# A cross-network kernel on one core: V2 spread by one-row transfers, M written in runs of 8 KB, the vectors in one load, chunk 1 loaded ahead of W2

## The chip, the core and the metric

The kernel runs on one core of a Trainium2 chip. The metric is device time in microseconds (us) of one execution. The six runs of the kernel before lie within 0.7% of each other. The span of a profile is a little shorter than the time (515.9 against 517.7 us in the profiled run of the kernel before, which was the fastest of its six). The profile counts 16 DMA engines on the core, which carry the transfers that SP (SyncE), ACT and POOL issue; a "DMA share" is the mean busy share of the 16, and a transfer has landed when its completion is reported. A run whose clock was throttled throughout is called slow, and such runs are not compared with others.

## The reference

A three-layer compressed interaction network over 1024 rows of 64 features and 16 embedding positions. Each layer multiplies every feature with every hidden channel and contracts the 64 x 64 products with a weight matrix:

```python
h = x0 = x                                   # [1024, 64, 16]
for i in range(3):
    z = einsum('bfe,bge->bfge', x0, h).reshape(B, 64 * 64, 16)
    y = einsum('oc,bce->boe', W[i], z) + b[i][None, :, None]     # 128 channels
    if i != 2: x_i, h = y[:, :64], y[:, 64:]
    else:      x_i = y
    xs.append(x_i)
out = sum(concatenate(xs, 1), 2) @ fc_w.T + fc_b
```

The kernel does not compute the third layer as such: only its weighted sum is wanted. It folds fc_w into W2, which gives a 64 x 64 matrix V2 (one matmul row over all of W2), folds V2 into W1, which gives M, a 64 x 64 x 64 tensor, and uses M, with its two feature axes added symmetrically, as 64 more weight columns beside those of layer 1. All is float32.

## The kernel before

TensorE (PE) contracts, VectorE (DVE) makes the products z, ScalarE (ACT) copies and squares. A chunk is 32 rows of the batch. V2 and M are made while chunks 0 to 3 run their first half (`half_contract(c, 0, j)`, the columns from W0); the second half (`half_contract(c, 1, j)`) needs the columns from M. The parts that matter:

```python
    # start: loads, all on SP's queue; eight semaphores for DMAs in turn
    load_xa(0); ...xw[0], xw[1]...            # chunk 0 and W0, 3 MB
    for k in range(2):
        nc.sync.dma_start(out=w2s[k], in_=w2t[k])      # W2, 2 x 1 MB
    load_chunk(1)                                      # 2 MB
    nc.sync.dma_start(out=w1s, in_=w1h)                # W1, 1 MB
    load_chunk(2)
    # ... 13 small loads of vectors on POOL (GpSimd)
    for j in range(2):
        half_contract(0, 0, j)
    load_chunk(3)
    # V2: column sums of W2 weighted with fc_w, on 4 partitions (0, 32, 64, 96)
    ...
    for to in halves:                                  # two transfers of 16 KB: 4 partitions -> 64, twice
        nc.scalar.dma_start(
            out=v2t[to],
            in_=v2r[0:128:32].rearrange("k n (o f) -> k (n o) f", f=F),
        )
    for j in range(2, NJ + 1):
        half_contract(0, 0, j)
    # ... chunk 1, first two tiles
    # M = V2 x W1, in m_sb [128, 4, 512]; written to memory as md[f1, f2, g], with wrapped copies of rows and columns
    def quarter(rows, first):
        return md[rows, first : first + 16, :].rearrange("r (m f) g -> r m (f g)", m=2)
    for n in range(2):
        at = 64 * n
        f0 = 16 * n
        nc.scalar.dma_start(out=quarter(slice(0, 64), f0), in_=m_sb[halves[n], n::2, :])
        nc.scalar.dma_start(out=quarter(slice(0, 64), 32 + f0), in_=m_sb[halves[1 - n], n::2, :])
        nc.sync.dma_start(out=quarter(slice(32, 64), 64 + f0), in_=m_sb[at + 32 : at + 64, n::2, :])
        nc.sync.dma_start(out=quarter(slice(64, 96), 32 + f0), in_=m_sb[64 - at : 96 - at, n::2, :])
        ...
    # ... chunks 2 and 3, first half
    # read back skewed (row f1 starts at column f1), in 1 KB and 256 B pieces, half on SP, half on ACT
    for half in range(2):
        ...
    nc.vector.tensor_tensor(w_all[:, 0:NT, 64:128], ms[:, 0], ms[:, 1], ALU.add)   # the weights from M
    load_chunk(4)
    for c in range(2, NF):                             # second half of chunks 2 and 3
        for j in range(NJ):
            half_contract(c, 1, j)
```

## Time and profile before

| | before |
|---|---|
| time, median of 6 runs | 519.22 us (517.73 to 520.98) |
| span of the profiled run | 515.9 us |
| PE busy | 495.8 us, 96% |
| PE idle at the start / for chunk 1 / for V2 / for the weights from M | 10.87 / 2.12 / 2.41 / 0.20 us |
| first weights from M used | 55.61 us |

A line of the chain view is a start, a duration and a piece of work; the chain is followed back from the last instruction, so a piece on it delayed the end. A line of an engine's timeline adds the matmul's shapes and, in brackets, how long the engine had been idle and what released it. PE counts each float32 matmul as two records, hence "x32" for 16 instructions. Lines such as L180 are lines of the kernel; the changed kernel has other line numbers for the same statements (L198 became L178, L302 became L275, L367 became L336, L159 became L139). The lines of this profile stand in the prediction below.

### The profile page before, as it was taken

To read this page: it belongs to the slowest core of one execution; us is meant where nothing else is said; L and a number is where in the kernel's file an instruction comes from. 1 tells how busy PE (TensorE), PEld (TensorE's weight loads), DVE (VectorE), ACT (ScalarE), POOL (GpSimd) and SP (SyncE) were. 2 spreads that over 40 slices of the span, in tenths; PEclk is the share of its full clock that TensorE was granted. 3 is DMA by queue.
4 is the path that set the end of the run, shared out by engine and by line. 5 is a ranking of instruction groups with operands and counts; after the bars stand their busy time and mean duration, and the time that the engine had idled before them with its cause. 6 is when DMAs were issued, how large, how long until landed. Compare 5 with 4: busy or idle time off the path is not lost.

```text
span 515.9 us, 3854 instructions
## 1 busy us (share of the span) xinstructions
PE 495.8 (96%) x1576; PEld 229.9 (45%) x1576; DVE 370.3 (72%) x224; ACT 81.5 (16%) x141; POOL 8.1 (2%) x23
## 2 busy tenths in 40 slices
PE   1889999999999999999999999999999999999996
PEld 0446754444544444444444444444444444444432
DVE  3698499999999995849577584957758495771103
ACT  1113114021311101111110111111011111100001
POOL 6000000000000000000000000000000000000000
PEclk9989999999999999999999999999999999999999
DMA  7977995344456544442324444232444421000000
GB/s 284 415 305 177 348 424 223 151 175 164 163 217 238 198 164 163 163 163 96 129 102 163 163 165 163 98 128 100 163 163 163 164 105 57 0 1 1 0 0 0
DMA packets 15167, 80.66 MB, mean 156 GB/s; under 512 B 4194, under 2 KB 4750, under 8 KB 5806
## 3 DMA queue, kind: packets, MB, share of 16 engines
q1 hardware_dynamic: 12626, 78.73, 39.6%
q10 hardware_dynamic: 2108, 1.61, 1.4%
q8 instruction: 12, 0.20, 0.1%
q0 software_dynamic: 416, 0.09, 0.1%
q14 instruction: 5, 0.04, 0.0%
HBM read 78.74 MB, written 1.64 MB: 156 GB/s over the span
## 4 chain that ended last, share of the span: by engine, by line
PE 93%; DMA 4%; DVE 1%; ACTq 1%; ACT 0%; issue 0%; SPq 0%; DVEq 0%
PE acc L180 75%; PE acc L198 9%; PE acc L185 5%; PE y L227 3%; DMA v2t<-v2r 3%; DMA xw<-in_xw 1%; DMA ms<-md 1%; DVE z L159 0%; PE pv L267 0%; PE pm L302 0%; PE po L431 0%; ACTq L360 0%; DVE w_all L367 0%; ACTq L274 0%; DVE uu L223 0%
## 5 line engine op out<-in xcount | busy, mean ns | idle before, releaser
L180 PE MATMUL acc<-z,w_all 128*128 128x512 f32 x896 | 392.0, 593 | 0.0
L159 DVE TENSOR_TENSOR z<-xa,xb 128x2048 f32<-128x2048 f32 x132 | 295.7, 2285 | 37.1 <-PE acc L180 28.3
L180 PEld LDWEIGHTS acc<-z,w_all 128*128 128x128 f32 x896 | 169.9, 190 | 214.0 <-issue 209.2
L198 PE MATMUL acc<-z,w_all 128*64 128x256 f32 x512 | 61.5, 400 | 13.2 <-DVE w_all L242 10.9
L222 ACT COPY q<-acc 64x512 f32<-64x512 f32 x28 | 16.3, 582 | 309.8 <-PE acc L185 309.4
L198 PEld LDWEIGHTS acc<-z,w_all 128*64 128x64 f32 x512 | 39.7, 144 | 35.6 <-DVE w_all L242 10.9
L230 DVE SCALAR_TENSOR_TENSOR uu<-y,cx,xx 128x512 f32<-128x512 f32 x16 | 11.9, 746 | 56.4 <-PE y L227 56.4
L223 DVE SCALAR_TENSOR_TENSOR uu<-acc,bh,q 64x512 f32<-64x512 f32 x28 | 20.7, 740 | 35.3 <-ACT q L222 34.8
L185 PE MATMUL acc<-zl,w_all 128*128 128x512 f32 x56 | 28.6, 592 | 0.0
L166 ACT ACTIVATE zl<-xa 64x512 f32<-64x512 f32 x34 | 21.3, 628 | 25.2 <-PE acc L198 17.7
L175 ACT COPY xx<-xa 64x512 f32<-64x512 f32 x32 | 19.6, 614 | 20.2 <-DVE uu L230 19.8
L234 DVE TENSOR_REDUCE acc<-uu 128x64 f32<-128x1024 f32 (+2 forms) x18 | 20.2, 1129 | 0.6
L171 ACT COPY zl<-xa 64x512 f32<-64x512 f32 x32 | 19.7, 615 | 0.4
L185 PEld LDWEIGHTS acc<-zl,w_all 128*128 128x128 f32 x56 | 10.6, 190 | 13.4 <-issue 13.4
L227 PE MATMUL y<-xx,bd 128*128 128x512 f32 x32 | 16.3, 595 | 0.0
L159 DVE TENSOR_TENSOR z<-xa,xw 128x2048 f32<-128x2048 f32 x4 | 9.1, 2285 | 8.2 <-DMA xw<-in_xw 8.2
L227 PEld LDWEIGHTS y<-xx,bd 128*128 128x128 f32 x32 | 6.0, 190 | 7.6 <-issue 7.6
L302 PE MATMUL pm<-w1s,v2t 64*64 64x512 f32 x16 | 3.0, 605 | 2.4 <-DMA v2t<-v2r 2.4
L437 ACT ACTIVATE res<-po,cst 2x480 f32<-2x480 f32 (+1 forms) x2 | 0.9, 465 | 25.2 <-PE po L431 25.2
L198 PE MATMUL acc<-zl,w_all 64*64 64x256 f32 (+1 forms) x32 | 4.9, 393 | 0.0
L204 ACT ACTIVATE hb<-acc,bh 128x256 f32<-128x256 f32 x4 | 1.9, 474 | 17.4 <-PE acc L198 17.4
L431 PE MATMUL po<-acc,ones 128*2 128x480 f32 (+1 forms) x8 | 2.2, 379 | 2.0 <-DVE acc L234 2.0
(46 smaller groups left out, 36.7 us busy)
## 6 DMA issues: line engine op xcount, KB each, us to landing
xa<-in_xra SPq DMA_DIRECT2D x34, 1024.0 KB, 4.7
xb<-in_xrb SPq DMA_DIRECT2D x33, 1024.0 KB, 7.2
w<-in_w2t SPq DMA_DIRECT2D x2, 1024.0 KB
xw<-in_xw SPq DMA_DIRECT2D x2, 512.0 KB, 8.2
xw<-in_xw SPq DMA_DIRECT2D x1, 1024.0 KB
w1s<-in_w1h SPq DMA_DIRECT2D x1, 1024.0 KB
md<-m_sb ACTq DMA_DIRECT2D x4, 256.0 KB, 5.1
w1x<-in_wx SPq DMA_DIRECT2D x1, 1024.0 KB, 9.9
```

The costliest lines, as they stand in the source:

```text
L159: nc.vector.tensor_tensor(z, xas[c], xbs[c][j].unsqueeze(1).to_broadcast([128, NI, N]), ALU.mult)
L166: nc.scalar.activation(zls[c][0:64], xas[c][0:64, 0, :], AF.Square)
L171: nc.scalar.copy(zls[c][64:128], xas[c][64:128, 0, :])
L175: nc.scalar.copy(xxs[c // 2][to], xas[c][to, 0, :])
L180: nc.tensor.matmul(accs[c], w_all[:, t, :], zs[c, j][:, i, :], start=(t == 0), stop=False)
L185: nc.tensor.matmul(accs[c], w_all[:, NT, :], zls[c], start=False, stop=True)
L198: nc.tensor.matmul(accs[c][halves[n]], w_all[rows, t, cols], z[rows, n * H2 : (n + 1) * H2], start=(t == 0), stop=(t == NT),)
L222: nc.scalar.copy(q, accs[c][64:128])
L223: nc.vector.scalar_tensor_tensor(uu, accs[c][0:64], bh1[0:64], q, ALU.add, ALU.mult)
L227: nc.tensor.matmul(ys[k], bd, xxs[k], start=True, stop=True)
L230: nc.vector.scalar_tensor_tensor(uus[k][:, 1, :], ys[k], cx, xxs[k], ALU.add, ALU.mult)
L234: nc.vector.tensor_reduce(acc[rows, parts, k, :], uus[k][rows, parts].rearrange("p k (b e) -> p k b e", e=E), AX.X, ALU.add,)
```

## The change

The intent: V2 reaches the other partitions sooner, by transfers that each use every DMA engine; M is laid out so that it leaves in runs of 8 KB with few transfers; thirteen small loads become one; and chunk 1 comes ahead of W2, so that PE has work. W1 is permuted on the host to suit. The core of the diff (the host's packing, the PE order of M's matmuls and the renaming of the read-back are cut):

```diff
-    nc.gpsimd.dma_start(out=fc2, in_=fc_w[0, 128:256].unsqueeze(1))
-    ...twelve more
+    vs = const_tile("vs", [128, NV])
+    nc.scalar.dma_start(out=vs, in_=vec)
...
+    load_chunk(1)
     for k in range(2):
         nc.sync.dma_start(out=w2s[k], in_=w2t[k])
-    load_chunk(1)
     nc.sync.dma_start(out=w1s, in_=w1h)
...
-    for j in range(2):
+    for j in range(NJ + 1):
         half_contract(0, 0, j)
+    keep_h1(0)
+    squares(1)
     load_chunk(3)
...
-    for to in halves:
+    for k in range(4):
         nc.scalar.dma_start(
-            out=v2t[to],
-            in_=v2r[0:128:32].rearrange("k n (o f) -> k (n o) f", f=F),
-        )
+            out=v2t[16 * k : 16 * k + 16],
+            in_=v2r[32 * k : 32 * k + 1].rearrange("k n (o f) -> k (n o) f", f=F),
+        )
+    nc.scalar.copy(v2t[halves[1]], v2t[halves[0]])
...
-    for j in range(2):
+    for j in range(3):
         half_contract(1, 0, j)
...
+    def m_ap(f1, f2, dims):
+        return bass.AP(tensor=md.tensor, offset=md.offset + f1 * row + f2 * F, ap=dims)
+    m_rows = m_sb.rearrange("p m c -> p (m c)")
+    nc.scalar.dma_start(out=m_ap(0, 0, [[32 * F, 2], [row, F], [1, 32 * F]]), in_=m_rows)
     nc.sync.dma_start(
-        out=md[68:96, 64:68, :].rearrange("r f g -> r (f g)"), in_=m_sb[4:32, 0, 0:256]
+        out=m_ap(32, 64, [[32 * row - 32 * F, 2], [row, 32], [1, 32 * F]]), in_=m_rows[32:96]
     )
+    nc.sync.dma_start(out=m_ap(64, 64, [[row, 4], [1, 32 * F]]), in_=m_rows[0:4])
+    nc.sync.dma_start(out=m_ap(68, 64, [[row, 28], [1, 4 * F]]), in_=m_rows[4:32, 0 : 4 * F])
```

In the read-back, the last small transfer moves from SP's queue to ACT's, and ACT's part comes ahead of its wait for chunk 2.

More of the change, by code (lines that the diff above doesn't have):

```diff
@@ L46, with cin_kernel @@
 NF = 4
+NV = 200
 @with_exitstack
-def cin_kernel(ctx, tc, xra, xrb, xw0, xw1, w0d, w1h, w2t, wx1, wx0, b0, b1, b2, fc_w, fc_b, out):
+def cin_kernel(ctx, tc, xra, xrb, xw0, xw1, w1h, w2t, wx1, wx0, vec, out):
     nc = tc.nc
@@ L70, in set_tile @@
         return setup.tile([128, NI * N], F32, tag="set", name=name)
-    fc2 = const_tile("fc2", [128, 1])
-    bh1 = const_tile("bh1", [128, 1])
-    bh2 = const_tile("bh2", [F, 1])
-    bcol = const_tile("bcol", [128, 2])
-    fcol = const_tile("fcol", [128, 2])
-    fcb = const_tile("fcb", [2, 1])
-    fcr = const_tile("fcr", [128, 128])
-    w0ds = const_tile("w0ds", [F, F])
-    b0c = b0.unsqueeze(1)
-    b1c = b1.unsqueeze(1)
-    nc.gpsimd.dma_start(out=fc2, in_=fc_w[0, 128:256].unsqueeze(1))
-    nc.gpsimd.dma_start(out=w0ds, in_=w0d)
-    for to in halves:
-        nc.gpsimd.dma_start(out=bh1[to], in_=b0c[64:128])
-    nc.gpsimd.dma_start(out=bh2, in_=b1c[64:128])
-    nc.gpsimd.dma_start(out=bcol[0:64, 0:1], in_=b0c[0:64])
-    nc.gpsimd.dma_start(out=bcol[64:128, 0:1], in_=b1c[0:64])
-    nc.gpsimd.dma_start(out=bcol[:, 1:2], in_=b2.unsqueeze(1))
-    for n in range(2):
-        nc.gpsimd.dma_start(
-            out=fcol[:, n : n + 1], in_=fc_w[0, n * 128 : (n + 1) * 128].unsqueeze(1)
-        )
-        nc.gpsimd.dma_start(out=fcb[n : n + 1], in_=fc_b.unsqueeze(1))
-    nc.gpsimd.dma_start(
-        out=fcr, in_=bass.AP(tensor=fc_w.tensor, offset=0, ap=[[0, 128], [1, 128]])
-    )
+    vs = const_tile("vs", [128, NV])
+    nc.scalar.dma_start(out=vs, in_=vec)
+    fc2, bh1, bh2 = vs[:, 0:1], vs[:, 1:2], vs[0:64, 2:3]
+    bcol, fcol, fcb = vs[:, 3:5], vs[:, 5:7], vs[0:2, 7:8]
+    w0ds, fcr = vs[0:64, 8:72], vs[:, 72:200]
     fv2 = const_tile("fv2", [128, 32])
-    nc.gpsimd.tensor_copy(fv2, fc2.to_broadcast([128, 32]))
+    nc.scalar.copy(fv2, fc2.to_broadcast([128, 32]))
     ones = const_tile("ones", [128, 2])
@@ L272, in cin_kernel @@
         nc.scalar.copy(v2r[:, n, :], pv)
-    for to in halves:
+    for k in range(4):
         nc.scalar.dma_start(
-            out=v2t[to],
-            in_=v2r[0:128:32].rearrange("k n (o f) -> k (n o) f", f=F),
-        )
-    for j in range(2, NJ + 1):
-        half_contract(0, 0, j)
-    keep_h1(0)
-    squares(1)
+            out=v2t[16 * k : 16 * k + 16],
+            in_=v2r[32 * k : 32 * k + 1].rearrange("k n (o f) -> k (n o) f", f=F),
+        )
+    nc.scalar.copy(v2t[halves[1]], v2t[halves[0]])
     new_acc(1, H2)
@@ L286, in cin_kernel @@
         product(1, j)
-    for j in range(2):
+    for j in range(3):
         half_contract(1, 0, j)
     m_sb = z_tile("m_sb")
-    pms = []
-    for m in range(0, NI, 2):
-        pms += [
-            ps.tile([128, N], F32, tag=("set", "y")[m // 2], name=f"pm_{m + n}") for n in range(2)
-        ]
+    pms = [ps.tile([128, N], F32, tag=("set", "y")[m // 2], name=f"pm_{m}") for m in range(NI)]
+    for m in (0, 1):
         for n in range(2):
             for h in range(2):
-                e = 2 * n + m // 2
@@ L302, in cin_kernel @@
                 nc.tensor.matmul(
-                    pms[m + n][halves[h ^ n]], v2t[halves[h]],
-                    w1s[halves[h], e * N : (e + 1) * N], start=True, stop=True,
-                )
-        for n in range(2):
-            nc.scalar.copy(m_sb[:, m + n, :], pms[m + n])
+                    pms[m + 2 * n][halves[h ^ n]], v2t[halves[h]],
+                    w1s[halves[h], (m + 2 * n) * N : (m + 2 * n + 1) * N], start=True, stop=True,
+                )
+    for m in range(NI):
+        nc.scalar.copy(m_sb[:, m, :], pms[m])
@@ L311, in cin_kernel @@
     md = dr.tile([EXT, EXT, F], F32, tag="md", name="md")
-    def quarter(rows, first):
-        return md[rows, first : first + 16, :].rearrange("r (m f) g -> r m (f g)", m=2)
-    for n in range(2):
-        at = 64 * n
-        f0 = 16 * n
-        nc.scalar.dma_start(out=quarter(slice(0, 64), f0), in_=m_sb[halves[n], n::2, :])
-        nc.scalar.dma_start(out=quarter(slice(0, 64), 32 + f0), in_=m_sb[halves[1 - n], n::2, :])
-        nc.sync.dma_start(out=quarter(slice(32, 64), 64 + f0), in_=m_sb[at + 32 : at + 64, n::2, :])
-        nc.sync.dma_start(out=quarter(slice(64, 96), 32 + f0), in_=m_sb[64 - at : 96 - at, n::2, :])
-        nc.sync.dma_start(out=quarter(slice(64, 68), 64 + f0), in_=m_sb[at : at + 4, n::2, :])
+    row = EXT * F
@@ L324, in cin_kernel @@
+    def m_ap(f1, f2, dims):
+        return bass.AP(tensor=md.tensor, offset=md.offset + f1 * row + f2 * F, ap=dims)
+    m_rows = m_sb.rearrange("p m c -> p (m c)")
+    nc.scalar.dma_start(out=m_ap(0, 0, [[32 * F, 2], [row, F], [1, 32 * F]]), in_=m_rows)
     nc.sync.dma_start(
-        out=md[68:96, 64:68, :].rearrange("r f g -> r (f g)"), in_=m_sb[4:32, 0, 0:256]
+        out=m_ap(32, 64, [[32 * row - 32 * F, 2], [row, 32], [1, 32 * F]]), in_=m_rows[32:96]
     )
-    for j in range(2, NJ + 1):
+    nc.sync.dma_start(out=m_ap(64, 64, [[row, 4], [1, 32 * F]]), in_=m_rows[0:4])
@@ L328, in cin_kernel @@
+    nc.sync.dma_start(out=m_ap(68, 64, [[row, 28], [1, 4 * F]]), in_=m_rows[4:32, 0 : 4 * F])
+    for j in range(3, NJ + 1):
         half_contract(1, 0, j)
@@ L339, in cin_kernel, with skewed @@
             half_contract(c, 0, j)
-    keep_h1(2)
-    ms = set_tile("ms").rearrange("p (v t g) -> p v t g", v=2, g=F)
-    row = EXT * F
-    def skewed(first, dims):
-        return bass.AP(
-            tensor=md.tensor, offset=md.offset + first, ap=[[row + F, F]] + dims
-        )
-    for half in range(2):
-        to = halves[half]
-        b = 16 * half + 4
-        queue = (nc.sync, nc.scalar)[half]
-        queue.dma_start(
-            out=ms[to, 0].rearrange("p (j i) g -> p j (i g)", i=NI),
-            in_=skewed(b * row, [[4 * row, NJ], [1, NI * F]]),
-        )
-        for i in range(NI):
-            queue.dma_start(
-                out=ms[to, 1].rearrange("p (j i) g -> p j i g", i=NI)[:, :, i, :],
-                in_=skewed(i * row + b * F, [[4 * F, NJ], [1, F]]),
-            )
-    nc.sync.dma_start(out=w_all[0:64, NT, 64:128], in_=skewed(0, [[1, F]]))
+    ms = set_tile("ms").rearrange("p (v t g) -> p v t g", v=2, g=F)
+    def skewed(f1, f2, dims):
+        at = len(dims) - 2
+        return m_ap(f1, f2, dims[:at] + [[row + F, F]] + dims[at:])
+    for half in range(2):
+        (nc.sync, nc.scalar)[half].dma_start(
+            out=ms[halves[half], 0].rearrange("p (j i) g -> p j (i g)", i=NI),
+            in_=skewed(16 * half + 4, 0, [[4 * row, NJ], [1, NI * F]]),
+        )
+    for i in range(NI):
+        for half in range(2):
+            queue = (nc.sync, nc.scalar)[half]
+            queue.dma_start(
+                out=ms[halves[half], 1].rearrange("p (j i) g -> p j i g", i=NI)[:, :, i, :],
+                in_=skewed(i, 16 * half + 4, [[4 * F, NJ], [1, F]]),
+            )
+    nc.scalar.dma_start(out=w_all[0:64, NT, 64:128], in_=m_ap(0, 0, [[row + F, F], [1, F]]))
+    keep_h1(2)
     keep_h1(3)
@@ L518 @@
     xw = np.stack([xrb[0], w0p], axis=2)
+    w1q = w1[64:].reshape(64, 2, 2, 16 * F)
+    w1q = np.stack([w1q[:, :, 0], w1q[:, ::-1, 1]], axis=2).transpose(1, 0, 2, 3).reshape(128, 32 * F)
+    b0, b1, b2 = (np.asarray(b) for b in (L0_rec_b0, L0_rec_b1, L0_rec_b2))
+    fc = np.asarray(L0_rec_fc_w)[0]
+    vec = np.concatenate([
+        np.stack([
+            fc[128:], np.tile(b0[64:], 2), np.tile(b1[64:], 2), np.concatenate([b0[:64], b1[:64]]),
+            b2, fc[:128], fc[128:], np.full(128, np.asarray(L0_rec_fc_b)[0]),
+        ], axis=1),
+        np.tile(w0[64:, np.arange(F), np.arange(F)].T, (2, 1)),
+        np.tile(fc[:128], (128, 1)),
+    ], axis=1)
     def summed(w):
@@ L528 @@
         "xw1": xw[:, 2:].reshape(128, 4, N),
-        "w0d": w0[64:, np.arange(F), np.arange(F)].transpose(1, 0),
-        "w1h": w1[64:].reshape(64, 2, 32 * F).transpose(1, 0, 2).reshape(128, 32 * F),
+        "w1h": w1q,
         "w2t": w2.transpose(0, 2, 1).reshape(128, 4, 2, 8 * F).transpose(2, 0, 1, 3).reshape(2, 128, 32 * F),
@@ L533 @@
         "wx0": summed(w0[:64]),
-        "b0": np.asarray(L0_rec_b0),
-        "b1": np.asarray(L0_rec_b1),
-        "b2": np.asarray(L0_rec_b2),
-        "fc_w": np.asarray(L0_rec_fc_w),
-        "fc_b": np.asarray(L0_rec_fc_b),
+        "vec": vec,
     }
```

## The prediction

> **What bounds the kernel now.** I read the page first, then the chain that ended last in order of time, the timeline of TensorE (PE), the waits, the time windows of the stretch that changes, and the DMA issues. On the page PE is busy 96% of the span: 495.8 of 515.9 us. The 20.1 us left are four gaps and the tail. The chain, where it passes through the stretch that the change touches:
>
> ```profile
> 1.19 6.89 DMA xw<-in_xw
> 8.18 2.29 DVE z L159
> ...
> 10.87 6.09 PE acc L198 x32
> 16.97 2.01 PE pv L267 x16
> 19.00 0.59 ACT v2r L272
> 19.62 1.15 ACTq L274
> 20.80 13.16 DMA v2t<-v2r
> 34.01 1.94 PE pm L302 x14
> 35.95 11.85 PE acc L198 x104
> ...
> 50.79 3.13 DMA ms<-md
> 54.24 1.24 DVE w_all L367
> 55.61 14.03 PE acc L198 x128
> ```
>
> First column is the start, second the duration. The only long piece that isn't PE work is the 13.16 us transfer of 2 x 16 KB of V2. The timeline of PE shows what of this PE really lost:
>
> ```profile
> 22.47 0.65 PE L198 MATMUL acc<-zl,w_all 64*64 64x256 f32 x4
> 25.25 5.36 PE L198 MATMUL acc<-z,w_all 128*64 128x256 f32 x32 [2.12 <-DVE z L159]
> 30.54 1.07 PE L302 MATMUL pm<-w1s,v2t 64*64 64x512 f32 x2
> 34.01 1.94 PE L302 MATMUL pm<-w1s,v2t 64*64 64x512 f32 x14 [2.41 <-DMA v2t<-v2r]
> ...
> 55.61 14.03 PE L198 MATMUL acc<-z,w_all 128*64 128x256 f32 x128 [0.20 <-DVE w_all L367]
> ```
>
> PE idles 2.12 us for chunk 1's product, 2.41 us for V2 and 0.20 us for the summed weights made from M (L367), besides 10.87 us at the start and some 4.5 us at the end. From 55.61 on it never waits until the tail. The 32 records at 25.25 take 5.36 us where the same 32 take 3.67 us at 18.87: 1.7 us lost to a slow clock. So **all that the change can win is 2.12 + 2.41 + 0.20 + 1.7 = 6.4 us, 1.2%**, plus little at the start. What it can lose has no such cap: M goes out to memory, comes back skewed, and becomes the weights that PE needs at 55.61, and there the slack was 0.2 us.
>
> **What the Trainium skill says.** (1) "DMA: Bandwidth & Descriptors", section "Why a DMA increments its semaphore by 16 and not by 1": a transfer runs on k engines, k being the largest number up to 16 that divides the count of the slowest dimension larger than 1 of both access patterns, as the instruction carries them, and on the SP and ACT queues it takes the lowest-numbered k. The same page, "Rules for kernel authors", warns that a small outermost dimension confines the whole transfer to that many engines. The trace agrees indirectly: V2's source has an outermost dimension of 4, so k = 4; two transfers of 64 rows are 128/4 = 32 rows for each of 4 engines, and 13.16 us / 32 = 0.41 us a row. (2) Same page, "Queues, rings and completion order": each engine alternates between queues packet by packet. A row then waits for one 8 KB packet of the loads: 8192 B over 414/16 = 25.9 GB/s is 0.32 us (414 GB/s is the mean over 19.5 to 34 us). That leaves 0.09 us for the row itself, so k = 4 fits; k = 16 would have taken some 3 us. (3) Same page, "Specifications": about 27 GiB/s an engine; the trace's loads run at 25.9 GB/s each. (4) "TensorE: Matmul & The Clock Gate", Part 1: an idle PE drops to half clock and needs about 3.4 us of work to recover. The window view agrees (last three columns: PE clock, DMA share, GB/s):
>
> ```profile
> 26.00:28.00 2.00, 2.00 (x14) 1.10 (x12) 2.00 (x2) 0.00 (x0) 0.00 (x0) 0.51 1.01 409
> 40.00:42.00 2.00, 2.00 (x20) 1.35 (x20) 2.00 (x2) 1.17 (x3) 0.00 (x0) 1.00 0.94 228
> ```
>
> The second line is the M write of the kernel before: all 16 engines near busy (0.94), 228 GB/s.
>
> **The change, part by part.**
>
> *Vectors in one load.* Thirteen small POOL transfers go, one of 100 KB on ACT comes. Between 5 and 9 us the DMA share was only 0.6 to 0.9, so the first operands may land up to 1 us earlier. I expect 0.5 us, and it is absorbed below.
>
> *Chunk 1 ahead of W2.* Landings before, read from who was released: first operands 8.1 us, the last of W2 17.9, chunk 1 at 20.3 and 22.9; so 2.5 us per MB. After: chunk 1 complete at 22.9 - 5.0 = 17.9, W2 at 22.9, W1 at 25.4. This removes the 2.12 us gap and most of the slow clock. PE does all of chunk 0 (10.9 to about 21), then waits about 1 us for W2.
>
> *V2.* Its sums end at 22.9 + 0.9, the copy at 24.4 (19.6 before, so 4.8 us later). Four transfers of 16 rows have k = 16: one row per engine each. Issuing takes 4 x 0.6 = 2.5 us, landing some 2.2 us more (my estimate: small transfers in this trace land in 2 to 4 us), the copy of the second half 0.2: M's matmuls start at about 29.3 instead of 34.0, while PE has three tiles of chunk 1 to do until 23.8 + 3 x 1.7 = 28.9. M is in SBUF at 29.3 + 1.9 + 1.5 = 32.7 instead of 37.2.
>
> *M written in 8 KB runs.* Here the built program decides. The big write is carried as out [2, 64, 2048], in [128, 1, 2048]; the second as out [2, 32, 2048], in [64, 1, 2048]. The outermost dimension of the destination is 2, hence **k = 2, and both on the same two engines**. Before it was [64, 2, 512] and [32, 2, 512], k = 16. Work per engine: 64 + 32 = 96 runs of 8 KB = 786 KB. At the loads' 25.9 GB/s that is 96 x 0.316 = 30.4 us. Writes in this trace were slower: 228 / (16 x 0.94) = 15.2 GB/s per busy engine with 2 KB runs, 135 ns a run against 79 ns at the loads' rate, so 56 ns extra a run. If that is per run, 8 KB takes 0.372 us and the write 35.7 us; if it is per byte, 52 us. I choose between the first two, 34 us. Start 32.7 + 1.5 for issue, 1 us for the loads still running, 1.5 us for the last receipt: M lies in memory at about 70.7 us, where before the reading back began at 45.56.
>
> *M read back.* The issue order is better than before (SP and ACT together; ACT issued at 48.11, waiting for PE), about 8.5 us until the last lands, then 1.4 us of DVE: weights ready at 70.7 + 9.9 = 80.6 us instead of 55.5. Chunk 4's loads are queued behind this on SP, but its products (5 us after the readback) are needed only after 14 us of PE work on these weights, so they cost nothing more.
>
> *PE meanwhile.* It runs out at about 49.8 us: 31.2 + 2.2 (rest of chunk 1) + 2 x 7.6 (chunks 2, 3) = 48.6, plus about 1 us. It stands still for about 31 us and restarts at half clock, losing about 2 us. The sum: 80.6 - 55.6 = 25.0, plus 2.0 = 27.0; all after 55.61 is PE-bound and moves as a block: **519.3 + 27.0 = 546 us**.
>
> **Rivals.** *A: the intended gain.* If the M write spreads over 16 engines after all (by a compiler that folds 2 x 64 into 128 on both sides, or a rule read wrongly), it takes 1.6 MB at 230 to 400 GB/s, 4 to 7 us, and weights are ready near 48, before PE needs them at 49.8. Then gaps of about 1 us (W2) and 0.4 us (V2) remain of the 6.4 us, with perhaps a slow clock: 514 to 517 us. Against it: the built program carries the 2 unfolded, and the V2 transfer before had the same kind of mismatch (64 rows against 4 x 16) and behaved like k = 4. I give it 12%.
>
> *B: the writes are bound per byte* at 15.2 GB/s an engine: 52 instead of 34 us, 564 us. For it: only that the two-kilobyte writes are the only writes seen. Against it: with 16 engines writing at once a limit of the memory would look the same, and two engines would not meet it.
>
> *C: only one of the two writes on two engines, or on different ones.* Then 64 runs count, not 96: 10 to 11 us less, about 535 us. Nothing in the trace tells; the skill's "lowest-numbered" speaks against it.
>
> *D: V2 remains slow.* It would delay M by up to 8 us. Against it: one row per engine and transfer, not 16. It would also be paid only because the M chain is now the bound.
>
> **Range and chances.** The core is k = 2 (88%), where the time spans 535 (C, or writes at load speed with quick receipts) to 562 (nearly per byte). Rival A lies wholly within 2% of 519.3 (508.9 to 529.7), and no reading gives over 1.2% gain. So faster 0.01, same 0.12, slower 0.87; 546 us, from 535 to 562.
>
> **What would show each step.** Right: the timeline of PE has no 2.12 us gap before chunk 1, M's matmuls start near 29 us, and one gap of 25 to 35 us ends near 80 us, released by the DVE sum of the M weights, with the half clock after it. The windows from 37 to 70 us show a DMA share near 0.12 (2 of 16) at 45 to 52 GB/s. The chain holds a piece "md<-m_sb" of over 30 us. V2 has a piece of 3 to 5 us. Wrong: a DMA share near 0.9 in the M write and reading back begun near 40 us mean rival A; a share of 0.12 at 30 GB/s means B; a much shorter stretch means C.

## The result, and the profile after

The changed kernel takes **544.92 us** (median of 6 runs, 542.88 to 545.25) against 519.22 us: a ratio of 1.0486, 95% interval 1.0458 to 1.0514, slower by 4.9%. Here and below a ratio is the mean time of one kernel's fast runs over that of the other's fast runs of the same rounds, so not quite the ratio of the medians quoted. The output is correct.

The chain that ended last, changed kernel, in order of time (start, duration, piece):

```profile
25.34 5.76 DMA v2t<-v2r
...
31.30 3.79 PE pm L275 x16
...
36.71 32.52 DMA md<-m_sb
69.23 0.02 issue
69.25 4.93 DMA ms<-md
74.20 4.35 DMA ms<-md
...
78.78 1.24 DVE w_all L336
80.02 0.04 issue
80.06 17.00 PE acc L178 x128
```

The 13.16 us of V2 have become 5.76 us, and in their place stands the write of M to memory, 32.52 us, which before was not on this chain at all. PE's timeline shows the two waits and two slow stretches:

```profile
22.62 5.40 PE L178 MATMUL acc<-z,w_all 128*64 128x256 f32 x48
31.30 3.79 PE L275 MATMUL pm<-w1s,v2t 64*64 64x512 f32 x16 [3.28 <-DMA v2t<-v2r]
...
52.17 0.65 PE L178 MATMUL acc<-zl,w_all 64*64 64x256 f32 x4
80.06 17.00 PE L178 MATMUL acc<-z,w_all 128*64 128x256 f32 x128 [27.24 <-DVE w_all L336]
```

The gap of 2.12 us for chunk 1 is gone. The wait for V2 is 3.28 us, not shorter than the 2.41 before, because V2's sums now come later; and after it M's matmuls run at half clock (3.79 us; granted clock 0.50 from 32 to 33 us). Then PE has no work from 52.8 to 80.06 us. The 128 records that took 14.03 us take 17.00: the restart costs 2.97 us.

The time windows of the write (first columns: stretch, its length, busy time of PE, weight loads, DVE, ACT and POOL; last three: PE clock, DMA share, GB/s):

```profile
40.00:65.00 25.00, 12.82 (x116) 7.67 (x112) 7.51 (x4) 1.80 (x4) 0.00 (x0) 0.81 0.13 53
```

A DMA share of 0.13 is two engines of sixteen; before, the same bytes went out at a share of 0.94 and 228 to 244 GB/s.

What follows moves as a block: from the end of those 128 records (69.64 us before, 97.06 after) to the end of the span it is 515.9 - 69.64 = 446.3 us before and 543.1 - 97.06 = 446.0 us after. The whole loss lies ahead of it: 24.45 us later start, 2.97 us slow clock, 27.4 us together, against 543.1 - 515.9 = 27.2 us of span. (The medians differ by 25.7 us, because the profiled run of the kernel before was its fastest.)

### The profile page after: what moved, and what is told of

It reads as the page before. It is cut to its first block, busy times and chain, and to the rows that moved or that the text cites. A ratio compares the mean times of both kernels' runs of the same rounds, so it can differ in the third digit from the quotient of the medians.

```text
span 543.1 us, 3825 instructions
## 1 busy us (share of the span) xinstructions
PE 497.3 (92%) x1576; PEld 229.0 (42%) x1576; DVE 370.5 (68%) x224; ACT 81.8 (15%) x143; POOL 0.8 (0%) x9
## 4 chain that ended last, share of the span: by engine, by line
PE 86%; DMA 10%; DVE 2%; ACT 0%; ACTq 0%; issue 0%; SPq 0%; DVEq 0%
PE acc L160 71%; PE acc L178 7%; DMA md<-m_sb 6%; PE acc L165 4%; PE y L207 3%; DMA ms<-md 2%; DVE z L139 2%; DMA xw<-in_xw 1%; DMA v2t<-v2r 1%; PE pm L275 1%; PE po L400 0%; PE pv L249 0%; ACTq L256 0%; DVE w_all L222 0%; DVE w_all L336 0%
## 5 line engine op out<-in xcount | busy, mean ns | idle before, releaser
L178 PE MATMUL acc<-z,w_all 128*64 128x256 f32 x512 | 62.3, 404 | 38.2 <-DVE w_all L336 27.2
L178 PEld LDWEIGHTS acc<-z,w_all 128*64 128x64 f32 x512 | 38.0, 146 | 63.9 <-DVE w_all L336 27.7
L203 DVE SCALAR_TENSOR_TENSOR uu<-acc,vs,q 64x512 f32<-64x512 f32 x28 | 20.7, 741 | 35.3 <-ACT q L202 34.8
L335 DVE MEMSET ms<- 64x64 f32 x1 | 0.1, 112 | 27.4 <-DMA ms<-md 27.4
L184 ACT ACTIVATE hb<-acc,vs 128x256 f32<-128x256 f32 x4 | 1.8, 471 | 48.5 <-DMA ms<-md 33.7
```

Source lines behind the costliest of these rows:

```text
L178: nc.tensor.matmul(accs[c][halves[n]], w_all[rows, t, cols], z[rows, n * H2 : (n + 1) * H2], start=(t == 0), stop=(t == NT),)
L203: nc.vector.scalar_tensor_tensor(uu, accs[c][0:64], bh1[0:64], q, ALU.add, ALU.mult)
```

## The experiments

**Theory.** The two big M writes are carried with a destination of outermost dimension 2, so both run on the same two DMA engines, and PE waits for the weights made from M. **Rivals.** The later V2 or the reordered read-back costs the time; or the two writes use different engines; or short or long runs matter rather than engines. Ratios are to the kernel before, of the same rounds.

### Both M writes on sixteen engines

```diff
-    nc.scalar.dma_start(out=m_ap(0, 0, [[32 * F, 2], [row, F], [1, 32 * F]]), in_=m_rows)
+    for h in range(2):
+        nc.scalar.dma_start(out=m_ap(0, 32 * h, [[row, F], [1, 32 * F]]), in_=m_rows[halves[h]])
-    nc.sync.dma_start(out=m_ap(32, 64, [[32 * row - 32 * F, 2], [row, 32], [1, 32 * F]]), in_=m_rows[32:96])
+    nc.sync.dma_start(out=m_ap(32, 64, [[row, 32], [1, 32 * F]]), in_=m_rows[32:64])
+    nc.sync.dma_start(out=m_ap(64, 32, [[row, 32], [1, 32 * F]]), in_=m_rows[64:96])
```

> The changed kernel with its two big M writes each cut in two, so that the destination's outermost dimension is 64 or 32 rows instead of 2; same bytes, same 8 KB runs. Theory (two DMA engines carry the whole write): the write falls from 32.5 us to 4 to 7 us plus some 3 us of issue and receipt, reading back begins at 43 to 46 us, the weights are ready at 54 to 57 us where PE runs out at 52.8 us; total 517 to 520 us. Rival (the read-back, its order or the later V2 costs the 25 us): it stays above 535 us.

Measured: 519.51 us (515.92 to 521.68), ratio 1.0007 (0.9956 to 1.0058). Chain, then PE's timeline:

```profile
38.46 6.94 DMA md<-m_sb
45.50 4.89 DMA ms<-md
```

```profile
56.09 14.03 PE L178 MATMUL acc<-z,w_all 128*64 128x256 f32 x128 [2.17 <-DVE w_all L336]
```

From the first issue of the write (36.91 us) to the first of the read-back (45.48) it is 8.6 us, where the change took 32.5. This one edit gives the whole loss back: the theory stands, the first rival falls. It also shows that the rest of the change is worth nothing as it stands, to half a per cent either way: PE still waits 3.6 us for V2 and 2.2 us for the weights. Nor do 8 KB runs help much once the engines are sixteen: the kernel before, with 2 KB runs in eleven transfers, took 8.85 us from first issue (36.71) to read-back (45.56).

### One of the two writes on sixteen engines

The edit above for SP's 0.5 MB alone, leaving 64 runs for each of the two engines:

> The changed kernel with only the smaller M write (SP's 0.5 MB) cut in two; the 1 MB write stays with outermost 2. Theory (both used the same two engines): 64 runs of 8 KB per engine remain of 96, a third less, about 21.7 us instead of 32.5; total about 534 us. Rival (the two writes ran on different pairs of engines, 64 runs being the longer): unchanged, 543 to 546 us.

And for ACT's 1 MB alone:

> The changed kernel with only the 1 MB M write cut in two; the 0.5 MB one stays with outermost 2. Theory: 32 runs per engine remain, about 11 to 12 us, weights near 60 us; total 522 to 525 us. Together with 96 and 64 runs the time should fall on a line of about 0.33 us per run.

Measured: 532.92 us (ratio 1.0268) and 536.05 us (1.0336). The write pieces of the two chains, one fence for each, and for the second run the last piece of its read-back:

```profile
36.79 24.45 DMA md<-m_sb
```

```profile
37.84 15.92 DMA md<-m_sb
...
59.50 10.03 DMA ms<-md
```

Both engines' runs of 8 KB, and the time from the first issue of the write to that of the read-back (from SP's and ACT's timelines):

| two-engine writes | runs per engine (worked out: two-engine plus spread ones) | us |
|---|---|---|
| none | 12 | 8.6 |
| SP's only | 32 + 8 = 40 | 17.9 |
| ACT's only | 64 + 4 = 68 | 24.5 |
| both (the change) | 96 | 32.5 |

These lie near a line, (32.5 - 8.6) / 84 = 0.285 us a run (an estimated 28.7 GB/s an engine, against 53 / 2 = 26.5 in the time window above), with the 17.9 us some 1.3 us above it. And both writes share the same two engines: with different pairs, taking SP's 32 runs away would have changed nothing, and it took 8 us off the write and some 12 us off the total. (The profile with 68 runs is of the slowest of five executions, 536.88 us, 4 us above the median, so the totals are the firmer evidence.) The first expectation was met in the total, though the write took 24.5 and not 21.7 us. The second was missed by 12 us: half of it by the write (17.9 instead of 11 to 12 us, mostly since I had left out the line's fixed 8.6 - 12 x 0.285 = 5.2 us and the 8 runs of the spread write), half by the read-back, which took 15.7 us (53.85 to 69.53) instead of the change's 9.3. I had not thought of that; the next two runs are about it.

### The M part alone

The kernel before, with W1's permutation, the order of M's matmuls and the two-engine writes of the change, nothing else. The core of the edit:

```diff
-    nc.scalar.dma_start(out=quarter(slice(0, 64), f0), in_=m_sb[halves[n], n::2, :])
-    ...ten more
+    nc.scalar.dma_start(out=m_ap(0, 0, [[32 * F, 2], [row, F], [1, 32 * F]]), in_=m_rows)
+    ...three more, as in the change
```

> The kernel before with the M part of the change alone (8 KB runs, destination outermost 2). Theory: the write takes the same 32.5 us from 37.2 us on, weights near 80 us where PE runs out at 55.4 us, restart at half clock; total 544 to 548 us. Rival (another part of the change is needed for the loss): under 530 us.

Measured: 555.57 us (554.21 to 556.43), ratio 1.0707: the M part alone loses more than the whole change. The write piece is the same to a tenth (38.16 to 70.75 us), but the read-back takes 17.3 us, and its last piece is

```profile
77.62 10.46 DMA ms<-md
```

On SP's timeline the loads of chunk 4, of a weight tile and of chunk 5 are issued from 74.87 us on, while ACT is still issuing its share of the read-back (71.56 to 78.26 us). In the changed kernel SP's first such load comes at 74.53 us, when ACT is at the last of its share (69.25 to 74.82 us). My expectation, 544 to 548 us, left this out.

### The loads behind the read-back

The kernel of the last section, with chunk 4, the weight tile and chunk 5 on ACT's queue instead of SP's, so behind the read-back:

```diff
-    load_chunk(4)
+    load_chunk(4, nc.scalar)
-    nc.sync.dma_start(out=w1x, in_=wx1)
+    nc.scalar.dma_start(out=w1x, in_=wx1)
-    load_chunk(5)
+    load_chunk(5, nc.scalar)
```

> The kernel before with the M part alone (555.6 us, 9 us more than the whole change), with the loads of chunks 4 and 5 and of one weight tile moved from SP's queue to ACT's, behind the read-back of M. Theory (the read-back's 256-byte rows on ACT's queue wait behind 8 KB packets that SP, already through with its own share, has sent): the read-back falls from 17.3 us to 9 to 11 us, total 546 to 549 us. Rival (the read-back is slow for another cause, such as lanes or cold memory): stays above 553 us.

Measured: 544.43 us (2 runs), ratio 1.0479, a little below the expected 546 to 549 us. The read-back takes 8.6 us (70.58 to 79.19), and its last piece is

```profile
76.70 2.46 DMA ms<-md
```

Eleven microseconds came back by moving five loads from one queue to another; the loads that came between the small pieces are the cause of the excess. For the 15.7 us of the run with 40 runs above the same cause is likely (SP's loads were issued from 57.75 us on, amid ACT's share of the read-back, 54.56 to 60.13 us), but it was not tested there.

### Two engines with runs of 2 KB

The two big writes cut by columns into four each, destination still outermost 2:

```diff
+    for m in range(NI):
+        nc.scalar.dma_start(out=m_ap(0, 8 * m, [[32 * F, 2], [row, F], [1, N]]), in_=m_sb[:, m, :])
+        # and the same for SP's write
```

> The changed kernel with the two big M writes cut by columns into four each: destination still outermost 2 (two engines), but runs of 2 KB, 384 per engine instead of 96. It settles the term of the prediction that was mis-sized (a fixed extra of 56 ns per run, read off the 2 KB writes of the kernel before). Theory A (a lone engine writes at its own byte rate, some 28 GB/s, whatever the run; the 15 GB/s before came from 16 engines writing at once): from M ready to the read-back again 32 to 35 us; total 543 to 550 us. Theory B (the extra is per run): 384 x 0.135 = 52 us for the write, total above 560 us.

Measured: 543.09 us (2 runs), ratio 1.0453; 34.5 us from the first issue (33.10) to the read-back (67.59), or 32.7 us from 34.91, when the last part of M was ready; here the first columns left before that.

```profile
44.00:60.00 16.00, 4.91 (x22) 2.48 (x24) 3.45 (x2) 3.88 (x7) 0.00 (x0) 0.58 0.14 52
```

(Issuing its four transfers held ACT for 19.5 us, 34.48 to 54.00, and PE waited 12.25 us for a tile that ACT makes. It cost nothing, since the weights from M came later still, at 78.5 us.) 52 GB/s with 2 KB runs, 53 with 8 KB: theory A. On two engines the length of a run does not matter, at least between these; the engines do. Then the 15.2 GB/s of a busy engine in the kernel before, which I took for a cost per run, belongs to sixteen engines writing at once: with 8 KB runs on sixteen engines it was 250 GB/s at a share of 0.89 (the first experiment, 38 to 44 us), so 17.6 GB/s each:

```profile
38.00:44.00 6.00, 6.00 (x56) 3.84 (x56) 6.00 (x4) 3.89 (x7) 0.00 (x0) 1.00 0.89 250
```

What limits it there was not tested.

### V2 with the loads out of the way

The first experiment's kernel, with chunks 2 and 3 loaded behind V2's transfers on ACT's queue:

```diff
-    load_chunk(2)
...
-    load_chunk(3)
...
     # after V2's four transfers
+    for c in (2, 3):
+        load_chunk(c, nc.scalar)
```

> The kernel with the M writes repaired (16 engines), and the loads of chunks 2 and 3 issued behind V2's four transfers on the same queue instead of ahead of them on the other. It asks why each 4 KB transfer of V2 took 5.9 us to land where I had estimated 2.2. Theory (they wait in engines full of 8 KB load packets): landing 2 to 3.5 us after issue, M's matmuls at about 29 us instead of 31.4, weights 2 us earlier; total 515 to 517.5 us against 519.5. Rival (it is the cost of a transfer between partitions, load or no load): landing stays near 5.9 us, total 518 to 521 us.

Measured: 515.62 us (515.35 to 516.07), ratio 0.9925 (0.9909 to 0.9941). The list of DMA issues (last number: median us from issue to landing), the changed kernel first:

```profile
v2t<-v2r ACTq DMA_DIRECT2D x4, 4.0 KB, 5.9
```

```profile
v2t<-v2r ACTq DMA_DIRECT2D x4, 4.0 KB, 1.8
```

A transfer of one row per engine lands in 1.8 us when little else moves (6 GB/s from 24 to 27 us) and in 5.9 us beside the loads (416 GB/s from 24 to 31 us); in the first experiment, which differs from this run by the edit alone, it was 6.1 us. M's matmuls start at 27.90 us instead of 31.45, without a wait. PE then waits 2.78 us for chunk 2, which was put last, so not all of it is won.

### V2 spread alone

The kernel before, with this and nothing else:

```diff
-    for to in halves:
-        nc.scalar.dma_start(out=v2t[to], in_=v2r[0:128:32].rearrange("k n (o f) -> k (n o) f", f=F))
+    for k in range(4):
+        nc.scalar.dma_start(
+            out=v2t[16 * k : 16 * k + 16],
+            in_=v2r[32 * k : 32 * k + 1].rearrange("k n (o f) -> k (n o) f", f=F),
+        )
+    nc.scalar.copy(v2t[halves[1]], v2t[halves[0]])
```

> The kernel before with V2 spread alone (four transfers of 16 rows, copy of the second half), all else as before. Theory (the spread is a gain by itself, off the critical path only in part): last landing near 27.5 us instead of 34, the 2.41 us gap ahead of M's matmuls closes, weights ready 4 to 6 us earlier than PE needs them; total 515.5 to 517.5 us. Rival (nothing won, as in the repaired change): 518.5 to 520 us.

Measured: 514.53 us (514.27 to 514.73), ratio 0.9903 (0.9885 to 0.9921), a little better than expected. In its PE timeline M's matmuls follow on chunk 1 without a wait, and the weights from M no longer hold PE up:

```profile
29.79 1.95 PE L303 MATMUL pm<-w1s,v2t 64*64 64x512 f32 x16
...
52.39 14.03 PE L198 MATMUL acc<-z,w_all 128*64 128x256 f32 x128
```

52.39 against 55.61 us is 3.2 us, about what the two profiled spans differ by (512.6 against 515.9); the medians differ by 4.9. Part of it may be the clock's: the gap before chunk 1 is still 2.11 us, but the half clock that followed it in the kernel before (5.36 us for 32 records) is absent, two tiles of 16 records taking 1.95 us each. This was not separated. This part of the change is good where W2 still comes first.

### The vectors alone, and the load order alone

The vectors' edit to the kernel before, with the matching packing on the host:

```diff
-    nc.gpsimd.dma_start(out=fc2, in_=fc_w[0, 128:256].unsqueeze(1))
-    ...twelve more
+    nc.scalar.dma_start(out=vs, in_=vec)
-    nc.gpsimd.tensor_copy(fv2, fc2.to_broadcast([128, 32]))
+    nc.scalar.copy(fv2, fc2.to_broadcast([128, 32]))
```

> The kernel before with the single load of all vectors alone. Theory: the first operands land about 0.5 us earlier (7.7 instead of 8.2 us, as in the changed kernel), but chunk 1 and V2 set the next waits; total 518 to 519.5 us. Rival (POOL's small transfers had slowed all loads up to chunk 1, which the whole start then follows): up to 1.5 us won, 517.5 us or less.

The vectors alone: 519.32 us, ratio 0.9998 (0.9977 to 1.0020). The first product starts at 7.75 us instead of 8.18 and chunk 1's at 21.37 instead of 22.90, but PE's wait for V2 grows from 2.41 to 3.74 us with another 1.13 ahead of it, and M's matmuls after it run at half clock (3.68 us). The gain is spent in the next wait.

The order's edit to the kernel before:

```diff
+    load_chunk(1)
     for k in range(2):
         nc.sync.dma_start(out=w2s[k], in_=w2t[k])
-    load_chunk(1)
...
-    for j in range(2):
+    for j in range(NJ + 1):
         half_contract(0, 0, j)          # all of chunk 0 ahead of V2's sums
...
-    for j in range(2):
+    for j in range(3):
         half_contract(1, 0, j)          # three tiles of chunk 1 ahead of M
```

> The kernel before with the load order alone (chunk 1 ahead of W2, PE's order of chunk 0, V2's sums and chunk 1 as in the changed kernel), V2 still by two transfers of 64 rows. Theory (the order closes the 2.1 us gap but puts V2's sums 3 to 4 us later, and V2's 13 us transfer then starts at 23 us): V2 lands at 33 to 36.5 us, PE waits 5 to 8 us there; total 520 to 524 us. Rival (order is a gain by itself): 515 to 518 us.

The order alone: 521.58 us (median of the five fast runs), ratio 1.0047 (1.0028 to 1.0066). One run of the six, and with it the profile, was slow (598.7 us, clock 0.85), so only the times are used; they fit the expectation, but where the time went was not seen in a fast run.

### V2 spread and the vectors together

The kernel before with these two edits, that of V2 and that of the vectors, and nothing else; order of loads and M as before.

```diff
+    nc.scalar.dma_start(out=vs, in_=vec)                     # for 13 loads on POOL
+    for k in range(4): nc.scalar.dma_start(out=v2t[16 * k : 16 * k + 16], in_=...)   # for two of 64 rows
```

> The two parts that should help, together: the kernel before with V2 spread and the vectors in one load; M written as before, loads in the order of before. Theory: the 4.9 us of V2 alone plus up to 0.5 us of the start; total 513.5 to 515 us, the fastest so far. Rival (the vectors' gain is absorbed by the wait for chunk 1, and ACT's extra work at the start delays it): 514.5 to 516 us.

Measured: **512.06 us** (511.91 to 512.26), ratio 0.9859 (0.9840 to 0.9879): faster than both kernels, and by more than expected.

```profile
27.74 1.95 PE L283 MATMUL pm<-w1s,v2t 64*64 64x512 f32 x16
...
50.33 14.03 PE L178 MATMUL acc<-z,w_all 128*64 128x256 f32 x128
```

With V2 out of the way, the earlier chunk 1 (its products start at 21.31 us, against 23.36 with V2 spread alone) is worth 514.53 - 512.06 = 2.5 us (the two are of different rounds; by their ratios 2.3 us), where alone it was worth nothing.

## Why the prediction was right, step by step

The direction, the cause and the time (546 against 544.92 us) were right. The steps:

| step | predicted | measured in the changed kernel |
|---|---|---|
| first operands earlier | 0.5 us | 8.18 to 7.71, 0.5 us |
| gap for chunk 1 | gone | gone |
| wait for W2 | about 1 us | none seen |
| copy of V2's sums ends | 24.4 us | 23.35 us |
| M's matmuls start / last | 29.3 / 1.9 us | 31.30 / 3.79 us |
| M in SBUF | 32.7 us | 36.7 us |
| write on two engines, to read-back | 38.0 us | 32.5 us |
| read-back and sum | 9.9 us | 10.8 us |
| weights ready | 80.6 us | 80.06 us |
| PE runs out of work | 49.8 us | 52.8 us |
| restart at half clock | 2.0 us | 2.97 us |

1. **Two engines** (k = 2 from the destination's outermost dimension): right. The share of 0.13 shows it, and cutting the transfers gives the loss back. The rule is that of the Trainium skill, "DMA: Bandwidth & Descriptors", section "Why a DMA increments its semaphore by 16 and not by 1"; here a destination of 2 x 64 rows against a source of 128 partitions was carried as it stood. That both writes shared the two engines is shown; which two they were is not. Rival A (12%) fell with the result, rival C (different engines) with the line over 32, 64 and 96 runs, rival B (bound per byte at 15.2 GB/s) with the 53 GB/s of two engines.
2. **The cost of a run** was mis-sized: I chose 34 us between 30.4 and 35.7. At 26.5 GB/s an engine 96 runs take 29.7 us, near the lower figure; the 56 ns "extra a run" does not exist on two engines. That is 4.3 of the 5.5 us by which the step came out short of my 38.0; the overheads around it were 32.5 - 29.7 = 2.8 us instead of 4.0.
3. **V2's landing** was mis-sized the other way: 2.2 us after the last issue in my estimate, 4.8 measured (26.27 to 31.10 us), because of the loads queued on the same engines. With the half clock after the wait this put M 4.0 us later than predicted. (The wait for one 8 KB packet a row that the prediction worked out fits V2's old transfer of 32 rows an engine, but it does not give the landing of a single row.) V2's sums came 1 us earlier than predicted: the single load of the vectors moved the loads behind it up by 1.5 us (chunk 1's products at 21.37 instead of 22.90 us in its run alone), where I had counted 0.5 us for the first operands only. The errors of the write and of M cancel almost, by luck; the total is closer than its terms deserve.
4. **The read-back** was right for this kernel, but the sentence that chunk 4's loads "cost nothing more" holds only because ACT's part happened to be issued in step with SP's. With other timing the read-back took 6 to 8 us longer; for the longer one the loads are shown to be the cause.
5. **The rest moves as a block**: right to 0.3 us.
6. **The intended gain**, rival A's 514 to 517 us, was also mis-sized: repaired, the change gives 519.51 us, not 514 to 517. The V2 wait and the half clock after it, and 2.2 us for the weights, take what the chunk 1 gap gave. The cap of 6.4 us was read from the fastest run of the kernel before; V2 spread and the vectors together won 7.2 us on the medians and 5.5 us between the profiled spans.

## What to carry to other kernels

Read a transfer's cost from the outermost dimension of both its patterns as the program carries them, before the length of its runs: two engines cost 24 us here, while 2 or 8 KB runs made no difference. Small transfers on a critical path should not share the engines with bulk loads issued around them; move the loads behind them in the same queue. And try the parts of a change alone and in pairs: here one part lost some 37 us, one won 4.9, one won nothing alone and 2.5 us beside another.

## What the Trainium skill lacked or had wrong

- "DMA: Bandwidth & Descriptors", on small transfers beside loads: by its round-robin ("Queues, rings and completion order") an engine drains a whole packet of one queue, typically 9 to 17 descriptors, before it turns to the next. It does not say how many 8 KB rows of a load make a packet, so the wait of one row stays open: 0.32 us if it is one, some 2.9 us if it is nine (estimates, from the prediction's 0.32 us a row and the page's 9). V2's old transfer, 0.41 us a row, favours one. Measured for a single row an engine was 5.9 us to landing beside the loads against 1.8 us with the loads behind, 4.1 us more; the page has no figure for this.
- The same page, on stores: it gives no trn2 rate for storing from SBUF to memory by length of run or number of engines. Measured: 53 GB/s on two engines with 8 KB runs and 52 with 2 KB; 250 GB/s on sixteen with 8 KB and 228 to 244 with 2 KB, so 26.5 GB/s an engine alone and some 15 to 18 when all write.
- "TensorE: Matmul & The Clock Gate", Part 1: it gives about 3.4 us of work to leave the half clock, counted in windows that run freely, so a restart can take longer than one. After 27 us without work PE lost 2.97 us, which makes an estimated 5.9 us at half clock (the granted clock was 0.50 up to 86 us, 6 us after the restart at 80.06); after the 2.12 us gap in the kernel before, it lost 1.7 us, an estimated 3.4 us, and after the 2.11 us gap with V2 spread alone nothing.
- "DMA: Bandwidth & Descriptors", rules for k: they were right for the case, and nothing was found wrong in them.
